# Raw rows into the tensor engine, with weights centred on chip, and a fourth block in the prologue of a two-layer attention and mixture-of-experts kernel

## The chip, the cores and the metric

The kernel runs on one NeuronCore of a Trainium2 chip. Times are device microseconds (us) of one execution. The kernel was run three times, and the median of such runs is what is compared. One further execution was recorded by the hardware profiler; its own time stands beside the median in the table below.

The engines are named as in the profile: PE is the tensor engine (PEld is its weight load), DVE the vector engine, ACT the scalar engine, POOL GpSimd, SP the sync engine. Transfers are issued by SP (the queue SPq) and by POOL.

## The reference

The input x has 128 graphs of 64 nodes with 256 features, in f32: 8192 rows. Two layers follow each other, each of an attention over a graph and a mixture of experts. Cut to what is computed (`ln` is a layer norm without gain and bias):

```python
for l in (0, 1):
    # attention inside each graph, adj is 0/1
    t  = ln(x)                                   # rows of 256
    Wh = t @ W[l]
    e  = (Wh @ a1[l])[:, :, None] + (Wh @ a2[l])[:, None, :]
    if l == 1: e = where(e > 0, e, 0.2 * e)
    p  = softmax(where(adj > 0, e, -9e15))
    x  = x + elu(p @ Wh)
    # mixture of experts: 8 experts, 2 for each row
    t  = ln(x)
    logits = t @ Wr[l]                           # l == 1: + bg + bias
    weights, chosen = softmax over the two largest logits
    act, hidden = (gelu, 256) if l == 0 else (relu, 512)
    f = sum over the two: weight * (act(t @ w1[e] + b1[e]) @ w2[e] + b2[e])
    x = x + (t + f if l == 0 else f)
```

## The kernel before, in words

*Tiling.* The 8192 rows are 16 blocks of 512. A block lies in memory as 128 partitions x 4 tiles (TT) x 256. A layer has 16 such blocks, so there are 32 block steps; block 3 of layer 0 is called FIRST.

*Attention of a block* is a generator, `attend` (L258), which is advanced a step at a time. It takes the statistics of the rows (`ln_stats` L221: mean and variance on DVE, then rs = (var + eps)^-0.5 on POOL, L230), turns adj into an additive mask on POOL (cap, L277), writes the normalised rows xn (`ln_apply` L233: nb = -mean * rs on DVE, L236, then one ACTIVATE for each of the four tiles, L238), transposes xn on PE (`transposed` L243, pt L249; the copies to SBUF are on DVE, L253, and ACT, L255), multiplies by the weights (pw, L288, copied to wh by ACT, L295), and forms scores (pe, L307), the softmax and its transpose (ee, exp, erc, pp, pT, L321 to L340), the product with wh (po, L346) and x + elu (xb, L360). The weights gw have 258 columns: 256 of W, and W @ a1 and W @ a2, which `make_gw` (L164) computes on chip from W and the attention vectors.

*Routing of a block* is a second generator, `route` (L400): statistics of xb, the normalised rows tn (L406), their transpose, the logits (pl, L417; lg, L426), the two largest (`largest` L367, used twice), an exp for the two weights (q), then the row's place in its expert's list (c1 to ix, L456 to L492; before the plan, pn), and eight list writes on POOL (L497), each of which scatters rows of tn with their place into the list of an expert in DRAM. In layer 0 the routine also turns xb into x + t in place, with rs1 = rs + 1 (L433), and stores it as `mid` from POOL's queue (L437); in layer 1 the same line stores xb to the output. The weighted sums of the experts are added to these stores later.

*Experts.* `Slots` works on slots of 256 list rows: `fetch` (L602) issues the load of list rows (xg, L609) and behind it the load of the expert's weights (wc, L651 to L659) on SP's queue; `x` (L669) transposes the rows (px L680, xT L684), `h` (L734) is the first product and its activation (ph L749, hT L757), `y` (L765) the second (py L777, ys L785), and a scatter of its rows to `res` (L791). In layer 1 `weighted` (L807) adds to the output in DRAM. The method `ahead` issues loads of weights ahead of their slot.

*Order.* The order on SP, PE, DVE and ACT is the program's order, written out by hand; only POOL's is chosen by a scheduler. The prologue (L885 to L922) loads blocks 0 to 2, and then advances several `chains` (L897) in turns, one step of each chain a turn; a tuple (turn, steps) tells from which turn on a chain takes part. `load(FIRST)` comes at turn 6, two further loads at turns 8 and 11, and `make_gw(1)` at turn 11:

```python
    chains = [
        (0, att(0)[3:] + [(r, 0)] * 10),
        (1, att(1)[2:] + [(r, 1)] * 10),
        (2, att(2) + [(r, 2)] * 10),
        (11, att(FIRST) + [(r, FIRST)] * 2),
        (20, [(a, FIRST + 1)] * 3),
    ]
```

Then `slots.fetch()` asks for the first list rows, and a loop (L924 to L978) runs over the block steps from FIRST on. An iteration t interleaves the attention of block t + 1 (`a(n)`), the routing of block t (`r(t)`) and four slots (`h`, `x`, `y`). At its first turn the loop gathers the second layer's expert biases (`gather_biases`, `put_biases`), and in the first two turns it fills the tails of the lists with pads (`rest_of_lists` L846, pads L850, eight DMAs for each layer). In layer 0, the lists hold three blocks before the first slot is worked on, so 24 list rows are written on POOL ahead of the first fetch.

Of the kernel before, what the change touches and what calls it, by code (L numbers as in the profile page):

```python
# [16 lines left out]
P = 128  # L17
# [18 lines left out]
def adj_ffn_kernel(  # L36
# [72 lines left out]
    sums_t = [mid_t, out_t]  # L109
# [14 lines left out]
    for g in range(2):  # L124
        r = slice(g * NG, (g + 1) * NG)
        nc.gpsimd.memset(same[r, r], 1.0)
    nhalf = const.tile([P, TT], F32, name="nhalf")
# [35 lines left out]

    def make_gw(l):  # L164
        wt = work.tile([P, KD, D], F32, tag="xt", name=f"wt{l}", bufs=2)
        for o in range(KD):
            pt = ps_c.tile([P, D], F32, tag="a", name=f"pwt{l}_{o}")
            for k in range(KD):
                nc.tensor.transpose(
                    pt[:, k * P : (k + 1) * P], gw[l][:, k, o * P : (o + 1) * P], ident  # L170
                )
            nc.scalar.copy(wt[:, o, :], pt)
        for k in range(KD):
            pa = ps_c.tile([P, 2], F32, tag="a", name=f"pa{l}_{k}")
            for o in range(KD):
                nc.tensor.matmul(
                    pa,
                    lhsT=wt[:, o, k * P : (k + 1) * P],
                    rhs=av[l][:, o, :],
                    start=(o == 0),  # L180
                    stop=(o == KD - 1),
                )
            nc.scalar.copy(gw[l][:, k, D : D + 2], pa)

# [9 lines left out]
    def counted(name, shape, pattern, base, mult):  # L194
        ti = work.tile(shape, I32, tag="cap", name=f"{name}_i")
        nc.gpsimd.iota(ti, pattern=pattern, base=base, channel_multiplier=mult)
        t = const.tile(shape, F32, name=name)
        nc.vector.tensor_copy(t, ti)
        return t
# [21 lines left out]
    def ln_stats(xb, name):  # L221
        st = small.tile([P, TT, 6], F32, tag="st", name=f"st_{name}")
        mv = small.tile([P, TT, 2], F32, tag="mv", name=f"mv_{name}", bufs=4)
# [5 lines left out]
        rs = small.tile([P, TT], F32, tag="rs", name=f"rs_{name}", bufs=4)  # L229
# [3 lines left out]
    def ln_apply(xb, stats, outs, name):  # L233
        mv, rs = stats
        nb = small.tile([P, TT], F32, tag="nb", name=f"nb_{name}", bufs=4)
# [22 lines left out]
    def attend(l, b, blk):  # L258
# [20 lines left out]
        xn = work.tile([P, TT, D], F32, tag="xn", name=f"xn_{name}", bufs=2)  # L279
        ln_apply(xs, stats, lambda t: xn[:, t, :], name)  # L280
        yield
        xt = transposed(xn, "xt", "a", name, l == 0 and b < FIRST)
        yield
        wh = work.tile([P, TT, D + 2], F32, tag="wh", name=f"wh_{name}")
        for t in range(TT):
# [9 lines left out]
            nc.scalar.copy(wh[:, t, :], pw)  # L295
# [71 lines left out]
    def largest(lg, name):  # L367

        mx = small.tile([P, TT], F32, tag="mx", name=f"mx_{name}", bufs=4)
# [8 lines left out]
        mo = small.tile([P, TT], F32, tag="mo", name=f"mo_{name}", bufs=4)  # L378
        nc.vector.tensor_reduce(mo, eq, AX.X, ALU.max)
        oh = small.tile([P, TT, E], F32, tag="oh", name=f"oh_{name}", bufs=4)  # L380
# [19 lines left out]
    def route(l, b, blk):  # L400
# [5 lines left out]
        tn = work.tile([P, TT, ROW[1]], F32, tag="tn", name=f"tn_{name}")  # L406
        nb = ln_apply(xb, stats, lambda t: tn[:, t, 0:D], name)
        if l == 0:
            rs1 = small.tile([P, TT], F32, tag="rs1", name=f"rs1_{name}")
            nc.vector.tensor_scalar(rs1, stats[1], 1.0, None, ALU.add)  # L410
        yield
        tT = transposed(tn, "tT", "r", name, l == 0 and b < FIRST)
# [12 lines left out]
        if l == 0:  # L425
            nc.vector.tensor_copy(lg, pl)  # L426
        else:
            nc.vector.tensor_tensor(lg, pl, gb2[:, 0:1, :].to_broadcast([P, TT, E]), ALU.add)
            nc.vector.tensor_tensor(lg, lg, gb2[:, 1:2, :].to_broadcast([P, TT, E]), ALU.add)
        m1, o1, oh1 = largest(lg, f"{name}a")  # L430
        if l == 0:
            for t in range(TT):
                nc.scalar.activation(  # L433
                    xb[:, t, :], xb[:, t, :], AF.Identity, bias=nb[:, t : t + 1],
                    scale=rs1[:, t : t + 1],
                )
        ins = nc.gpsimd.dma_start(out=sums_t[l][b], in_=xb)  # L437
        if l == 1:
            unordered("sums", ins)
            summed.append(ins)  # L440
# [9 lines left out]
        nc.scalar.activation(q, q, AF.Exp)  # L450
        yield
# [379 lines left out]
    def load_block(l, b, first=None):  # L831

        xs = work.tile([P, TT, D], F32, tag="xs", name=f"xs{l}_{b}")
# [40 lines left out]
    def r(i, n=1):  # L874
# [14 lines left out]
    a(0, 2)  # L889
    make_gw(0)  # L890
    a(0)
    a(1, 2)
# [3 lines left out]
    att = lambda b: [(a, b)] * 9 + [(a, b, 2), (a, b)]  # L896
    chains = [  # L897
        (0, att(0)[3:] + [(r, 0)] * 10),
        (1, att(1)[2:] + [(r, 1)] * 10),
        (2, att(2) + [(r, 2)] * 10),  # L900
        (11, att(FIRST) + [(r, FIRST)] * 2),
        (20, [(a, FIRST + 1)] * 3),
    ]
    turn = 0
    while any(c for _, c in chains):
# [4 lines left out]
        if turn == 2:  # L910
# [3 lines left out]
            tb0 = gather_biases(0)  # L914
        if turn == 5:
            put_biases(0, tb0)
            load_gw(1)
        if turn in (6, 8, 11):
            load(FIRST + (turn - 6) // 2)
        if turn == 11:  # L920
            make_gw(1)
        turn += 1  # L922
    slots.fetch()
    for t in range(FIRST, len(blks)):  # L924
# [4 lines left out]
        if t == FIRST:  # L929
            put_biases(1, gather_biases(1))  # L930
            rest_of_lists(0)
        if t == FIRST + 1:
            rest_of_lists(1)
# [11 lines left out]
        a(n)  # L945
        r(t)
# [20 lines left out]
        r(n)  # L967
        y()
        a(t + 2)
# [5 lines left out]
        r(n)  # L975
# [60 lines left out]
```

## Time and profile before

| | |
|---|---|
| median of 3 runs | 1467.6 us |
| lowest and highest of them | 1464.61 and 1468.28 us |
| the profiled execution | 1464.47 us |
| its span | 1462.6 us |
| its mean granted TensorE clock | 0.956 |
| busy: PE, PEld | 1264.9 us (86%), 1082.9 us (74%) |
| busy: DVE, ACT, POOL | 885.6 us (61%), 670.3 us (46%), 767.8 us (52%) |
| ACTIVATE xn (L238), 128 times | 66.4 us of ACT, 589 ns each |
| ACTIVATE tn (L238), 128 times | 66.4 us of ACT, 589 ns each |
| copy to wh (L295), 128 times | 47.7 us of ACT, 374 ns each |
| list writes (L497), 256 times | 249.5 us of POOL, 975 ns each |

The span is the time from the first to the last recorded instruction. A busy share is an average over the prologue, the loop of layer 0, the loop of layer 1 and the end. The page cuts the span into 40 slices of 36.6 us and gives a digit for each engine: the tenths of the slice in which it was busy. The row PEclk gives in the same way the clock that PE was granted, in tenths of full speed. In an answer of the trace, a line such as "94.31 3.36 PE L346 MATMUL ... x8 [0.21 <-ACT pT_bd L340]" reads: starts at 94.31 us, lasts 3.36 us, line 346, eight of them, after 0.21 us of idle time that ended with an instruction of ACT on pT_bd at line 340. The suffix _g marks a tile of attention, _r one of routing, _s one of a slot.

### The profile page before, as it was taken

The page shows a single profiled execution, that of the slowest core. Times are in us where ns is not written, and L with a number is a line of the kernel's source. Part 1 is how long each engine was busy: PE and PEld are TensorE (multiplying, and loading weights), DVE is VectorE, ACT ScalarE, POOL GpSimd, SP SyncE. Part 2 cuts the span into 40 slices and gives each one's busy share as a digit, 9 for nine tenths or more (in the row PEclk, how much of TensorE's full clock was granted, in tenths as well). Part 3 has the DMA queues.
Part 4 walks back from the last instruction along what each step waited for, and adds up shares of the span by engine and source line. Part 5 has one row for each costly group of instructions (what it writes and reads, how often), then busy time and mean ns, then how long its engine had stood idle before and what let it go on. Part 6 is the DMA issues. An engine that isn't in the chain of part 4 may idle for free. (4 is left out here: it accounts for less than half of the span.)

```text
span 1462.6 us, 22822 instructions
## 1 busy us (share of the span) xinstructions
PE 1264.9 (86%) x6436; PEld 1082.9 (74%) x6436; DVE 885.6 (61%) x3404; ACT 670.3 (46%) x1567; POOL 767.8 (52%) x742
## 2 busy tenths in 40 slices
PE   6646789889989888888889999899988998899996
PEld 4534677777777777777778887777877787688885
DVE  3663777776677678677766655666566655423332
ACT  5523556546655554545444444344444443233232
POOL 3261566656565555555563654555645465544333
PEclk9766999989999999999999999999999999999999
DMA  4228766697666779777786987898877778987773
GB/s 128 83 98 266 240 209 219 210 279 233 214 216 210 268 253 271 260 240 235 240 254 183 265 238 205 220 263 223 228 195 215 209 193 212 241 248 215 214 178 57
DMA packets 267199, 315.42 MB, mean 216 GB/s; under 512 B 41400, under 2 KB 224319, under 8 KB 267073
## 3 DMA queue, kind: packets, MB, share of 16 engines
q1 hardware_dynamic: 222240, 227.80, 51.3%
q0 software_dynamic: 44832, 86.17, 22.0%
q8 instruction: 51, 0.84, 0.2%
q14 instruction: 76, 0.61, 0.1%
HBM read 215.03 MB, written 102.51 MB: 217 GB/s over the span
## 5 line engine op out<-in xcount | busy, mean ns | idle before, releaser
L749 PE MATMUL ph_s<-xT_s,wc_s 128*128 128x256 f32 x1760 | 418.9, 388 | 71.1 <-DVE xT_s L684 49.3
L749 PEld LDWEIGHTS ph_s<-xT_s,wc_s 128*128 128x128 f32 x1760 | 333.4, 193 | 135.1 <-DVE xT_s L684 66.6
L777 PE MATMUL py_s<-wc_s,hT_s 128*128 128x256 f32 x1760 | 417.1, 387 | 14.9 <-issue 14.6
L777 PEld LDWEIGHTS py_s<-wc_s,hT_s 128*128 128x128 f32 x1760 | 331.4, 193 | 59.9 <-issue 17.2
L820 POOL DMA_INDIRECT out_dram<-ys_s,to_s x142 | 223.1, 1571 | 273.2 <-ACT ys_s L817 170.3
L497 POOL DMA_INDIRECT lists<-tn_r,ix_r x256 | 249.5, 975 | 110.9 <-issue 66.1
L757 ACT ACTIVATE hT_s<-ph_s,wc_s 128x256 f32<-128x256 f32 x440 | 182.3, 469 | 176.8 <-PE ph_s L749 88.1
L785 DVE TENSOR_TENSOR ys_s<-py_s,wc_s 128x512 f32<-128x512 f32 x149 | 102.9, 691 | 196.1 <-PE py_s L777 184.5
L791 POOL DMA_INDIRECT res<-ys_s,to_s x156 | 159.0, 1019 | 117.4 <-DVE ys_s L785 51.6
L684 DVE COPY xT_s<-px_s 128x512 f32<-128x512 f32 x149 | 102.3, 686 | 118.1 <-PE px_s L680 118.1
L817 ACT ACTIVATE ys_s<-ys_s,cf_s 128x256 f32<-128x256 f32 x142 | 64.1, 499 | 141.1 <-DVE ys_s L785 134.8
L288 PE MATMUL pw_g<-gw,xt_g 128*128 128x258 f32 x512 | 125.5, 395 | 1.7 <-ACT wh_g L295 1.3
L288 PEld LDWEIGHTS pw_g<-gw,xt_g 128*128 128x128 f32 x512 | 95.8, 196 | 22.8 <-ACT xt_g L255 6.3
L238 ACT ACTIVATE xn_g<-xs,nb_g,rs_g 128x256 f32<-128x256 f32 x128 | 66.4, 589 | 82.0 <-DVE nb_g L236 82.0
L238 ACT ACTIVATE tn_r<-xb_g,nb_r,rs_r 128x256 f32<-128x256 f32 x128 | 66.4, 589 | 66.8 <-DVE nb_r L236 66.8
L680 PE MATMUL px_s<-ident,xg_s 128*128 128x128 f32 x596 | 90.9, 276 | 0.5 <-DMA xg_s<-lists 0.5
L680 PEld LDWEIGHTS px_s<-ident,xg_s 128*128 128x128 f32 x596 | 74.9, 145 | 13.0 <-DMA xg_s<-lists 0.6
L277 POOL TENSOR_SCALAR cap_g<-adj 128x256 f32<-128x256 int32 x32 | 35.7, 1117 | 91.6 <-DMA adj<-in_adj_dram 90.2
L346 PE MATMUL po_g<-wh_g,pT_bd 128*128 128x256 f32 x256 | 69.0, 417 | 7.4 <-ACT pT_bd L340 5.8
L295 ACT COPY wh_g<-pw_g 128x258 f32<-128x258 f32 x128 | 47.7, 374 | 54.2 <-PE pw_g L288 53.2
L417 PEld LDWEIGHTS pl_r<-rw,xt_r 128*128 128x128 f32 x512 | 68.1, 207 | 2.9 <-DVE xt_r L253 0.6
L230 POOL TENSOR_TENSOR rs_r<-ve_r,nhalf 128x4 f32<-128x4 f32 x32 | 38.3, 1198 | 57.1 <-DVE ve_r L228 50.4
(474 smaller groups left out, 1597.8 us busy)
## 6 DMA issues: line engine op xcount, KB each, us to landing
wc_s<-in_w_dram SPq DMA_DIRECT2D x142, 512.0 KB, 4.3
wc_s<-in_w_dram SPq DMA_DIRECT2D x156, 256.0 KB, 3.9
xg_s<-lists SPq DMA_DIRECT2D x78, 258.0 KB, 4.3
xg_s<-lists SPq DMA_DIRECT2D x71, 260.0 KB, 4.4
yb<-res SPq DMA_DIRECT2D x16, 1024.0 KB, 10.5
wc_s<-bcat SPq DMA_DIRECT2D x78, 129.0 KB, 3.8
wc_s<-bcat SPq DMA_DIRECT2D x71, 130.0 KB, 5.3
xs<-in_x_dram SPq DMA_DIRECT2D x16, 512.0 KB, 6.1
```

Source lines behind the costliest of these rows:

```text
L238: nc.scalar.activation(outs(t), xb[:, t, :], AF.Identity, bias=nb[:, t : t + 1], scale=rs[:, t : t + 1])
L288: nc.tensor.matmul(pw, lhsT=xt[:, k, t * P : (t + 1) * P], rhs=gw[l][:, k, :], start=(k == 0), stop=(k == KD - 1),)
L346: nc.tensor.matmul(po[h][:, j, :], lhsT=pT[:, 2 * h + j, :], rhs=wh[:, 2 * h + j, 0:D], start=True, stop=True,)
L497: ins = nc.gpsimd.indirect_dma_start(out=lists[l], out_offset=bass.IndirectOffsetOnAxis(ap=ix[:, k, t : t + 1], axis=0), in_=tn[:, t, 0 : ...
L680: nc.tensor.transpose(px[:, c, t * P : (t + 1) * P], xg[:, t, c * P : (c + 1) * P], ident)
L684: nc.vector.tensor_copy(xT, px)
L749: nc.tensor.matmul(ph[:, j, :], lhsT=wc[:, o : o + P], rhs=xT[:, c, :], start=(c == 0), stop=(c == KD - 1),)
L757: nc.scalar.activation(hT[:, f + j, :], ph[:, j, :], AF.Gelu if l == 0 else AF.Relu, bias=wc[:, OB1[l] + f + j : OB1[l] + f + j + 1],)
L777: nc.tensor.matmul(py[:, t, :], lhsT=hT[:, f, t * P : (t + 1) * P], rhs=wc[:, O2[l] + f * D : O2[l] + (f + 1) * D], start=(f == 0), stop=( ...
L785: nc.vector.tensor_tensor(ys, py, wc[:, OB2[l] : OB1[l]].unsqueeze(1).to_broadcast([P, ST, D]), ALU.add)
L791: ins = nc.gpsimd.indirect_dma_start(out=res[sl["part"]], out_offset=self.row(sl, t), in_=ys[:, t, :], in_offset=None, bounds_check=2 * N - 1,
L820: ins = nc.gpsimd.indirect_dma_start(out=out, out_offset=self.row(sl, t), in_=ys[:, t, :], in_offset=None, compute_op=ALU.add,)
```

## The change

A layer norm followed by a product, ((x - mean) * rs) @ W, equals rs * (x @ (W - column means of W)), since subtracting the row's mean from x is the same as taking each column's mean out of W. The changed kernel uses this form for the attention's product and for the router's.

- A new function `centred` takes the column means out of a weight: two matmuls with a constant matrix `mean` that holds 1/256, and a subtraction on DVE for each of the two halves of the weight. It is applied to gw (with its two columns of attention vectors) and to rw, in both layers.
- In `attend` xn and its nb are gone; the raw rows xs are transposed. The copy to wh becomes an ACTIVATE that multiplies by rs.
- In `route` the raw rows xb are transposed; the logits are multiplied by rs when they are read from PSUM. tn is still made, since the lists hold it, but after the logits. The update of xb and the store of mid come after the exp of q.
- Some small tiles have six buffers instead of four; the integer tile of `counted` uses another tag.
- Block FIRST of layer 0 is loaded with the first three, into a buffer of tag yb, which layer 0 otherwise leaves unused.
- The prologue's chains are written anew: their steps are shorter, blocks 1 and 2 go together, block 3 begins at turn 8 and block 4 at turn 12. The biases of layer 1, the pads of both layers, `make_gw(1)` and the centring of layer 1 are in the prologue, and `slots.ahead()` follows the first fetch.
- In the loop the steps are arranged to the new lengths of `attend` (11 instead of 12) and `route` (11 instead of 10).

```diff
+    mean = const.tile([P, P], F32, name="mean")
+    nc.gpsimd.memset(mean, 1.0 / D)
...
+    def centred(w, n, name):
+        pm = ps_c.tile([P, n], F32, tag="a", name=f"pm_{name}")
+        for k in range(KD):
+            nc.tensor.matmul(pm, lhsT=mean, rhs=w[:, k, :], start=(k == 0), stop=(k == KD - 1))
+        for k in range(KD):
+            nc.vector.tensor_tensor(w[:, k, :], w[:, k, :], pm, ALU.subtract)
...
     def make_gw(l):
...
+        centred(gw[l], D + 2, f"gw{l}")
...
     def attend(l, b, blk):
...
-        xn = work.tile([P, TT, D], F32, tag="xn", name=f"xn_{name}", bufs=2)
-        ln_apply(xs, stats, lambda t: xn[:, t, :], name)
-        yield
-        xt = transposed(xn, "xt", "a", name, l == 0 and b < FIRST)
+        xt = transposed(xs, "xt", "a", name, l == 0 and b < FIRST)
...
-            nc.scalar.copy(wh[:, t, :], pw)
+            nc.scalar.activation(wh[:, t, :], pw, AF.Identity, scale=stats[1][:, t : t + 1])
...
     def route(l, b, blk):
...
-        tn = work.tile([P, TT, ROW[1]], F32, tag="tn", name=f"tn_{name}")
-        nb = ln_apply(xb, stats, lambda t: tn[:, t, 0:D], name)
-        if l == 0:
-            rs1 = small.tile([P, TT], F32, tag="rs1", name=f"rs1_{name}")
-            nc.vector.tensor_scalar(rs1, stats[1], 1.0, None, ALU.add)
-        yield
-        tT = transposed(tn, "tT", "r", name, l == 0 and b < FIRST)
+        tT = transposed(xb, "tT", "r", name, l == 0 and b < FIRST)
...
-        if l == 0:
-            nc.vector.tensor_copy(lg, pl)
-        else:
-            nc.vector.tensor_tensor(lg, pl, gb2[:, 0:1, :].to_broadcast([P, TT, E]), ALU.add)
-            nc.vector.tensor_tensor(lg, lg, gb2[:, 1:2, :].to_broadcast([P, TT, E]), ALU.add)
+        nc.vector.tensor_tensor(
+            lg, pl, stats[1].unsqueeze(2).to_broadcast([P, TT, E]), ALU.mult
+        )
+        for i in range(2 * l):
+            nc.vector.tensor_tensor(
+                lg, lg, gb2[:, i : i + 1, :].to_broadcast([P, TT, E]), ALU.add
+            )
         m1, o1, oh1 = largest(lg, f"{name}a")
-        if l == 0:
-            for t in range(TT):
-                nc.scalar.activation(
-                    xb[:, t, :], xb[:, t, :], AF.Identity, bias=nb[:, t : t + 1],
-                    scale=rs1[:, t : t + 1],
-                )
-        ins = nc.gpsimd.dma_start(out=sums_t[l][b], in_=xb)
+        yield
+        tn = work.tile([P, TT, ROW[1]], F32, tag="tn", name=f"tn_{name}")
+        nb = ln_apply(xb, stats, lambda t: tn[:, t, 0:D], name)
         if l == 1:
+            ins = nc.gpsimd.dma_start(out=out_t[b], in_=xb)
             unordered("sums", ins)
             summed.append(ins)
         yield
...
         nc.scalar.activation(q, q, AF.Exp)
+        yield
+        if l == 0:
+            rs1 = small.tile([P, TT], F32, tag="rs1", name=f"rs1_{name}")
+            nc.vector.tensor_scalar(rs1, stats[1], 1.0, None, ALU.add)
+            for t in range(TT):
+                nc.scalar.activation(
+                    xb[:, t, :], xb[:, t, :], AF.Identity, bias=nb[:, t : t + 1],
+                    scale=rs1[:, t : t + 1],
+                )
+            nc.gpsimd.dma_start(out=mid_t[b], in_=xb)
         yield
...
+        tag, bufs = ("yb", 2) if l == 0 and b == FIRST else ("xs", 3)
+        xs = work.tile([P, TT, D], F32, tag=tag, name=f"xs{l}_{b}", bufs=bufs)
...
     load_router()
-    a(0, 2)
+    load(FIRST)
+    a(0, 3)
     make_gw(0)
-    a(0)
-    a(1, 2)
+    centred(rw[0], E, "rw0")
+    a(1, 3)
...
-    att = lambda b: [(a, b)] * 9 + [(a, b, 2), (a, b)]
+    att = lambda b: [(a, b, 2)] + [(a, b)] * 6 + [(a, b, 2), (a, b)]
+    rou = lambda b: [(r, b, 2), (r, b, 2)] + [(r, b)] * 6
     chains = [
-        (0, att(0)[3:] + [(r, 0)] * 10),
-        (1, att(1)[2:] + [(r, 1)] * 10),
-        (2, att(2) + [(r, 2)] * 10),
-        (11, att(FIRST) + [(r, FIRST)] * 2),
-        (20, [(a, FIRST + 1)] * 3),
+        (0, att(0)[2:] + rou(0)),
+        (2, att(1)[2:] + rou(1)),
+        (2, att(2) + rou(2)),
+        (8, att(3) + [(r, 3)]),
+        (12, [(a, 4, 2)]),
     ]
...
         if turn == 5:
-            put_biases(0, tb0)
+            put_biases(0, tb)
             load_gw(1)
-        if turn in (6, 8, 11):
-            load(FIRST + (turn - 6) // 2)
+            tb = gather_biases(1)
+            put_biases(1, tb)
+        if turn in (6, 8):
+            load(4 + (turn - 6) // 2)
         if turn == 11:
             make_gw(1)
+            centred(rw[1], E, "rw1")
+            for l in range(2):
+                rest_of_lists(l)
         turn += 1
+    r(2)
     slots.fetch()
+    slots.ahead()
     for t in range(FIRST, len(blks)):
...
-        if t == FIRST:
-            put_biases(1, gather_biases(1))
-            rest_of_lists(0)
-        if t == FIRST + 1:
-            rest_of_lists(1)
...
         if more:
             x()
         a(n)
+        r(t)
         r(t)
...
         r(n)
+        r(t)
         y()
-        a(t + 2)
         r(t)
         r(t)
         y()
         slots.fetch()
         x()
-        r(n)
         r(t)
```

More of the change, by code (lines that the diff above doesn't have):

```diff
@@ L108, in adj_ffn_kernel @@
     res_t = [r.rearrange("(b t p k) d -> b p t (k d)", t=TT, p=P, k=2) for r in res]
-    sums_t = [mid_t, out_t]
     def part(b):
@@ L194, in counted @@
     def counted(name, shape, pattern, base, mult):
-        ti = work.tile(shape, I32, tag="cap", name=f"{name}_i")
+        ti = work.tile(shape, I32, tag="ee", name=f"{name}_i")
         nc.gpsimd.iota(ti, pattern=pattern, base=base, channel_multiplier=mult)
@@ L222, in ln_stats @@
         st = small.tile([P, TT, 6], F32, tag="st", name=f"st_{name}")
-        mv = small.tile([P, TT, 2], F32, tag="mv", name=f"mv_{name}", bufs=4)
+        mv = small.tile([P, TT, 2], F32, tag="mv", name=f"mv_{name}", bufs=6)
         for t in range(TT):
@@ L228, in ln_stats @@
         nc.vector.tensor_scalar(ve, mv[:, :, 1], LN_EPS, None, ALU.add)
-        rs = small.tile([P, TT], F32, tag="rs", name=f"rs_{name}", bufs=4)
+        rs = small.tile([P, TT], F32, tag="rs", name=f"rs_{name}", bufs=6)
         nc.gpsimd.tensor_tensor(rs, ve, nhalf, ALU.pow)
@@ L234, in ln_apply @@
         mv, rs = stats
-        nb = small.tile([P, TT], F32, tag="nb", name=f"nb_{name}", bufs=4)
+        nb = small.tile([P, TT], F32, tag="nb", name=f"nb_{name}", bufs=6)
         nc.vector.scalar_tensor_tensor(nb, mv[:, :, 0], -1.0, rs, ALU.mult, ALU.mult)
@@ L367, in largest @@
     def largest(lg, name):
-        mx = small.tile([P, TT], F32, tag="mx", name=f"mx_{name}", bufs=4)
+        mx = small.tile([P, TT], F32, tag="mx", name=f"mx_{name}", bufs=6)
         nc.vector.tensor_reduce(mx, lg, AX.X, ALU.max)
@@ L377, in largest @@
         )
-        mo = small.tile([P, TT], F32, tag="mo", name=f"mo_{name}", bufs=4)
+        mo = small.tile([P, TT], F32, tag="mo", name=f"mo_{name}", bufs=6)
         nc.vector.tensor_reduce(mo, eq, AX.X, ALU.max)
-        oh = small.tile([P, TT, E], F32, tag="oh", name=f"oh_{name}", bufs=4)
+        oh = small.tile([P, TT, E], F32, tag="oh", name=f"oh_{name}", bufs=6)
         nc.vector.tensor_tensor(
@@ L831, in load_block @@
     def load_block(l, b, first=None):
-        xs = work.tile([P, TT, D], F32, tag="xs", name=f"xs{l}_{b}")
+        tag, bufs = ("yb", 2) if l == 0 and b == FIRST else ("xs", 3)
+        xs = work.tile([P, TT, D], F32, tag=tag, name=f"xs{l}_{b}", bufs=bufs)
         yb = None
@@ L913, in adj_ffn_kernel @@
             snum = counted("snum", [P, SF], [[1, SF]], 0, 0)
-            tb0 = gather_biases(0)
+            tb = gather_biases(0)
         if turn == 5:
-            put_biases(0, tb0)
+            put_biases(0, tb)
             load_gw(1)
-        if turn in (6, 8, 11):
-            load(FIRST + (turn - 6) // 2)
+            tb = gather_biases(1)
+            put_biases(1, tb)
+        if turn in (6, 8):
+            load(4 + (turn - 6) // 2)
         if turn == 11:
             make_gw(1)
+            centred(rw[1], E, "rw1")
+            for l in range(2):
+                rest_of_lists(l)
         turn += 1
+    r(2)
     slots.fetch()
+    slots.ahead()
     for t in range(FIRST, len(blks)):
```

## The prediction, made before the changed kernel had run

> **What bounds the kernel now.** I read the page's share of busy time and its 40 slices first, then busy time by window, then the tensor engine's waits, then the order of time around the longest of them.
>
> ```profile
> PE 1264.9 (86%) x6436; PEld 1082.9 (74%) x6436; DVE 885.6 (61%) x3404; ACT 670.3 (46%) x1567; POOL 767.8 (52%) x742
> ...
> PE   6646789889989888888889999899988998899996
> ...
> PEclk9766999989999999999999999999999999999999
> ```
>
> PE is the bound, but not at the start: the first four slices (146 us) hold digits 6, 6, 4, 6 and a granted clock that falls to 0.6. The windows say it in figures (columns: window, length, then busy us of PE, PEld, DVE, ACT, POOL, clock, DMA share, GB/s):
>
> ```profile
> 60.00:80.00 20.00, 14.64 (x62) 11.97 (x63) 13.53 (x69) 10.58 (x24) 5.92 (x6) 0.57 0.21 66
> 80.00:100.00 20.00, 10.78 (x51) 8.73 (x49) 11.00 (x51) 6.18 (x19) 15.43 (x17) 0.74 0.36 126
> 100.00:120.00 20.00, 8.67 (x29) 6.02 (x30) 8.89 (x44) 5.92 (x13) 9.22 (x10) 0.57 0.53 159
> 120.00:140.00 20.00, 10.02 (x45) 7.50 (x43) 9.57 (x34) 5.84 (x19) 3.00 (x3) 0.61 0.94 280
> ```
>
> No engine is full here; the prologue is a chain of waits. Of the 198 us in which PE is idle (1462.6 - 1264.9), 65 lie before 200 us, by the same windows added up from 0. Its waits up to 200 us (line waited at, what it waited for, total, times, longest):
>
> ```profile
> PE pt_g L249 <- ACT xn_g L238: 26.1, 9, 13.6
> ...
> PE ph_s L749 <- DMA wc_s<-in_w_dram: 6.4, 1, 6.4
> PE pwt L169 <- DMA gw<-in_gnn_w_dram: 6.1, 1, 6.1
> ```
>
> 26.1 is also the total of that first wait over the whole run: after 200 us PE never waits for a normalised row. The place of the longest two, in order of time:
>
> ```profile
> 94.31 3.36 PE L346 MATMUL po_g<-wh_g,pT_bd 128*128 128x256 f32 x8 [0.21 <-ACT pT_bd L340]
> 111.28 2.80 PE L249 MATMUL pt_g<-ident,xn_g 128*128 128x128 f32 x8 [13.60 <-ACT xn_g L238]
> ...
> 123.41 0.63 PE L680 MATMUL px_s<-ident,xg_s 128*128 128x128 f32 x4
> ...
> 138.66 3.38 PE L749 MATMUL ph_s<-xT_s,wc_s 128*128 128x256 f32 x8 [6.40 <-DMA wc_s<-in_w_dram]
> ```
>
> Why 13.6: the scale rs of block 4 is ready to be made at 102.4, but POOL is writing list rows, 24 of them from 77.72 to 109.32 at 0.96 + 0.30 us each, and rs stands behind. Why 6.4: the sync queue issues the first expert's weights at 134.15, behind a bias gather that holds it to 123.15 and eight pads of 9.29 us:
>
> ```profile
> 110.99 3.07 SPq L609 DMA_DIRECT2D xg_s<-lists  x4
> ...
> 123.65 9.29 SPq L850 DMA_DIRECT2D lists<-pad  x8
> 134.15 0.40 SPq L651 DMA_DIRECT2D wc_s<-in_w_dram  x1
> ```
>
> **The change, step by step.** The sum is made against the profiled execution (1464.47 us, of it 1462.6 span); the median of the runs is 1467.6, 3.1 more, and that is added at the end. PE's order in the loop is the same list of matmuls as before; only the prologue's order differs.
>
> *Loop.* Removed: 128 ACTIVATEs (xn, 589 ns, 66.4 us of ACT) and 32 nb (152 ns) on DVE. Added: the copy to wh (374 ns) becomes a scaled ACTIVATE from PSUM. No row shows that; bounds are 374 and 589 (L238, two operands from SBUF), nearest is L757 (PSUM, one pointer operand, 469 ns): +95 ns x 128 = 12 us of ACT. PE hides both: a tile of pw takes it 0.87 us, in which ACT spends 0.5 us waiting, and after 200 us no xn wait is left to win. Without that cover it would be 0.4 us per block. The router's scale replaces a copy of 0.19 us by a multiply of the same size; nb_r now stands ahead of ys and erc on DVE, at most 0.15 us in the roughly 20 blocks where PE waits for the softmax: +2. The update of xb and the store of mid move two steps later; mid is read again only in layer 1, and the transposes no longer wait for tn, so nobody is late. Loop: +2 us (0 to +5; the freed ACT could give back up to 5).
>
> *Start.* The first transposes need only x: 5.2 instead of 9.81 us. But the first weights must be centred before any pw: 4 matmuls like pw (395 ns, 1.6) and 2 subtractions like L321 (0.42, 0.85), after the attention vectors. So pw starts at about 12.7 (12.43 now). Gained is what followed: block 1's transposes no longer wait for xn, so pe of block 0 comes at 17.5 instead of 21.0, pw of block 2 at 27 instead of 35.9, the first router logits at 44 instead of 55.5.
>
> *The list chain.* The first expert row can be fetched only after 24 list rows are written, and they start with ix of block 0. In the new DVE order ix of block 0 stands behind nearly all else: from xb of block 0 (35.2) come 36.6 us of DVE work (5 statistics of 2.4, for r0, g3, r1, r2, g4; 5 half routings of 1.35 to 1.7; xb of three blocks at 2.6; the rest in pieces under 1 us; 2.75 for ix itself). DVE stalls on top: it must wait for block 1's logits, which queue on PE behind block 3's transposes, these behind a PSUM bank that DVE frees late (4 us); for the centring of layer 1, which POOL's and ACT's queues don't hide because DVE's subtraction stands in line behind sm of block 3 (pw, ACT's xb and xt copies, wt, scores, 4 matmuls: 7.5 us); some 2 more. 35.2 + 36.6 + 13.5 = 85.3, with signal hops 86, against 77.7 now. Bounds: 76 with half those stalls and some overlap, 92 with twice the centring stall.
>
> [...] after the 13.6 us gap the half-rate matmuls last from 111.28 to 119.5 (pw 5.67 instead of 3.83), and the windows from 60 to 140 stay at 0.57 to 0.74. I take the rows: 3.42, 1.7, 3.42, and 86.
>
> From there POOL: 24 x 1.27, two stores of mid (0.85) and one rs (1.05) = 33.3, end at 119.3 (109.3 now). Fetch 1.7 later as now, landing 4.4 us after (section 6), so px at 125.4 (123.4 now). Block 4's rs is ahead of the list rows in the new POOL order, so the 13.6 us wait goes, but PE arrives early and waits for xg: that is the next late thing.
>
> *The weights.* They follow xg directly: 119.3 + 1.7 + 3.1 + 1.6, landing 4.3 later at 130. From px to the first ph the chain of pp, po takes 8.8 (123.4 to 132.25 now): 134. So ph starts at 134 instead of 138.66: -5. The 6.4 us are won, 1.4 are lost by the later lists. Pads, bias gather and loads now stand earlier on the sync queue, behind the load of block 5 (its buffer comes free near 43 us); 16 pads of 1.16 end near 62, long before the first list row that waits for them.
>
> *Second stall.* At 171.97 PE waits 5.2 us for xn of block 6. That goes; but the next ph needs weights issued at 172.29, landing 4.3 later, and ran at 179.81: at most 3.2 is won, and mid of block 3 now lies among the list rows (-0.9): -2.3. Clock recovered in both stalls: -2 (0 to -4).
>
> Sum: +2 - 5 - 2.3 - 2 = -7.3, so 1457 for the profiled execution and 1460 for the median. The ends: list start at 76 gives -10 more (1450), at 92 gives +6 (1466).
>
> **Rivals.** *Dense prologue and freed ACT*: list start near 76, ACT's 54 us help the loop by 5: 1460 - 10 - 5 = 1445 at best, 1449 as its middle. For it: no engine is above 77% in any window from 60 to 140 us. Against: DVE alone has 36.6 us of work in that stretch. *Traded*: the new wait for xg takes the place of both old ones, list start at 89: 1464 to 1471, like now; for it speaks that POOL's 31 us of list rows are unchanged. *Slower*: the centring of layer 1 sits in DVE's line; if its stall is 20 us instead of 7.5, list start is 98, ph at 146 and the second gain can't cover it: 1460 + 13 = 1473. It decides from a list start of 95 on. Against it: make_gw alone took 2.5 us at 60 us.
>
> **How the numbers follow.** Likeliest (1453 to 1463): 0.47. Dense: 0.19. Traded: 0.20. Slower: 0.14. Three runs spread by 3.7 us, so 0.3% (4.4 us) is about what can be told. Below 1463.2 lie the first two: faster 0.66; traded is mostly same: 0.19; slower with a piece of traded: 0.15. The range 1446 to 1472 leaves out half of the slower case and a third of the dense one.
>
> **What would show it.** Right: no wait for xn; the first list row near 86 and the last near 119; px waiting for xg by 8 to 14 us; no wait for weights; first ph near 134; loop iterations as long as before (38 us); DVE idle for 7 us ahead of the subtraction of layer 1. Wrong: a first list row before 80 or after 92, or loop waits of ph and pp that differ by more than 5 us in sum.

## The result, and the profile after

The changed kernel takes 1463.02 us (median of 20 runs, 1458.29 to 1468.07), the kernel before 1467.19 us (20 runs, 1462.14 to 1471.29). The ratio is 0.9971, interval 0.9960 to 0.9982: 4.2 us faster, between 2.6 and 5.9. The profiled executions stand closer together, 1464.47 and 1462.60 us, since that of before lies 2.7 us below its own median and that of after 0.4 us below. Where traces are subtracted below, this is why they sum to less than the medians.

The page of the changed kernel, the rows that answer to those of before:

```profile
PE 1264.8 (87%) x6452; PEld 1088.8 (75%) x6452; DVE 887.3 (61%) x3396; ACT 627.8 (43%) x1439; POOL 765.9 (52%) x743
...
PE   7746788889899888888899999889988898899996
...
PEclk9757999999999998999999999999999999999999
```

ACT lost 42.5 us of work (670.3 to 627.8) and PE is as busy as before: the freed ACT time did not shorten PE's (e2 below tells what it was worth). The copy to wh, now scaled, takes 476 ns, close to the 469 taken for it. The first four slices of PE read 7, 7, 4, 6 instead of 6, 6, 4, 6. The windows from 60 to 140 us (same columns as before):

```profile
60.00:80.00 20.00, 17.12 (x72) 14.59 (x72) 8.97 (x44) 7.86 (x20) 2.18 (x2) 0.67 0.30 90
80.00:100.00 20.00, 7.53 (x33) 6.06 (x31) 14.69 (x74) 9.33 (x25) 12.34 (x13) 0.67 0.26 92
100.00:120.00 20.00, 9.10 (x44) 7.70 (x44) 8.98 (x42) 6.00 (x17) 14.81 (x16) 0.67 0.34 119
120.00:140.00 20.00, 13.01 (x48) 10.39 (x48) 11.03 (x40) 5.34 (x11) 1.63 (x2) 0.66 0.85 250
```

PE is busy 46.8 us of these 80, against 44.1 before: the prologue is still a chain of waits, only with other names. PE's waits up to 200 us:

```profile
PE px_s L691 <- DMA xg_s<-lists: 10.2, 2, 8.1
PE pw_g L296 <- DVE xt_g L264: 10.1, 1, 10.1
PE ph_s L760 <- DVE xT_s L695: 7.7, 4, 5.4
PE pp_g L345 <- DVE c_r L467: 6.9, 1, 6.9
```

No row for xn and none for the weights is left. In their place PE waits for DVE's line (10.1 and 6.9) and, as the last long wait ahead of the first ph, for the first list rows (8.1). The places where the prediction put numbers, on POOL, SP and PE:

```profile
85.65 1.12 POOL L508 DMA_INDIRECT lists<-tn_r,ix_r  x1 [1.17 <-DVE l_r L444]
...
117.71 0.96 POOL L508 DMA_INDIRECT lists<-tn_r,ix_r  x1 [0.30 <-issue]
```

```profile
46.58 13.20 SPq L863 DMA_DIRECT2D lists<-pad  x16
...
120.62 3.09 SPq L620 DMA_DIRECT2D xg_s<-lists  x4
124.26 0.38 SPq L662 DMA_DIRECT2D wc_s<-in_w_dram  x1
```

```profile
123.48 1.12 PE L691 MATMUL px_s<-ident,xg_s 128*128 128x128 f32 x4 [8.10 <-DMA xg_s<-lists]
...
131.33 2.94 PE L760 MATMUL ph_s<-xT_s,wc_s 128*128 128x256 f32 x8
```

The weights follow the first fetch by 3.6 us (23.2 before: 110.99 to 134.15), the first ph runs at 131.33 instead of 138.66. The first list row, however, is written at 85.65 instead of 77.72.

### The profile page after: what moved, and what is told of

The parts are those of the page before. It is cut to its first block, busy times and chain, and to the rows that moved or that the text cites. A ratio compares the mean times of both kernels' runs of the same rounds, so it can differ in the third digit from the quotient of the medians.

```text
span 1460.7 us, 22860 instructions
## 1 busy us (share of the span) xinstructions
PE 1264.8 (87%) x6452; PEld 1088.8 (75%) x6452; DVE 887.3 (61%) x3396; ACT 627.8 (43%) x1439; POOL 765.9 (52%) x743
## 3 DMA queue, kind: packets, MB, share of 16 engines
q0 software_dynamic: 44832, 86.17, 22.2%
## 5 line engine op out<-in xcount | busy, mean ns | idle before, releaser
L788 PE MATMUL py_s<-wc_s,hT_s 128*128 128x256 f32 x1760 | 421.5, 390 | 14.3 <-issue 11.2
L296 PE MATMUL pw_g<-gw,xt_g 128*128 128x258 f32 x512 | 124.0, 395 | 12.5 <-DVE xt_g L264 10.1
L691 PE MATMUL px_s<-ident,xg_s 128*128 128x128 f32 x596 | 92.2, 278 | 10.2 <-DMA xg_s<-lists 10.2
L303 ACT ACTIVATE wh_g<-pw_g,rs_g 128x258 f32<-128x258 f32 x128 | 60.6, 476 | 65.7 <-PE pw_g L296 64.3
L345 PE MATMUL pp_g<-ident,ee_g 128*64 128x128 f32 x128 | 20.8, 289 | 52.1 <-DVE ee_g L341 26.5
```

The lines of the kernel that those rows point to most:

```text
L296: nc.tensor.matmul(pw, lhsT=xt[:, k, t * P : (t + 1) * P], rhs=gw[l][:, k, :], start=(k == 0), stop=(k == KD - 1),)
L691: nc.tensor.transpose(px[:, c, t * P : (t + 1) * P], xg[:, t, c * P : (c + 1) * P], ident)
L788: nc.tensor.matmul(py[:, t, :], lhsT=hT[:, f, t * P : (t + 1) * P], rhs=wc[:, O2[l] + f * D : O2[l] + (f + 1) * D], start=(f == 0), stop=( ...
```

## The experiments

All ratios are to the kernel before, run on the same chip in the same stretch; the changed kernel's is 0.9971.

### One half alone: the prologue, the loop

*e1* has the changed prologue and the loop of before (shown as the difference between the two forms of the functions; the kernel holds both and picks by block):

```diff
     # attend, blocks from 4 on
+        xn = work.tile([P, TT, D], F32, tag="xn", name=f"xn_{name}", bufs=2)
+        ln_apply(xs, stats, lambda t: xn[:, t, :], name)
+        yield
-        xt = transposed(xs, "xt", "a", name, l == 0 and b < FIRST)
+        xt = transposed(xn, "xt", "a", name, l == 0 and b < FIRST)
...
-            nc.scalar.activation(wh[:, t, :], pw, AF.Identity, scale=stats[1][:, t : t + 1])
+            nc.scalar.copy(wh[:, t, :], pw)
...
     # route, blocks from 3 on: tn first, as before; the loop's order as before
```

> The changed kernel's prologue (weights centred, raw rows, block 3 early, pads and biases early) with the loop of before: from block 4's attention and block 3's routing on, xn and tn are made first and transposed, as before. Theory (the gain is all in the prologue and the loop gives 2 to 4 us back): first ph near 131, loop as before, 5 to 8 us faster than before, so 1460. Rival (the ACT time freed in the loop is the gain): within 2 us of before.

Measured: 0.9924 (0.9906 to 0.9943), 1457.96 against 1469.26 us, 11 us faster. The gain is in the prologue, and it is larger without the new loop: 11 us where 5 to 8 were expected. The place of the first ph was missed as well: it ran at 136.0, because block 4's xn was waited for once more (12.4 us).

*e2* is the other half: prologue of before, loop of the change, both layers' weights centred at the head of the loop:

```diff
     # attend for blocks 0 to 3 and route for blocks 0 to 2 as before
...
         if t == FIRST:
             put_biases(1, gather_biases(1))
             rest_of_lists(0)
+            for l in range(2):
+                centred(gw[l], D + 2, f"gw{l}")
+                centred(rw[l], E, f"rw{l}")
```

> The prologue of before (its order, its loads, xn and tn for blocks 0 to 2, xn for block 3) with the loop of the changed kernel on raw rows; the weights of both layers are centred at the head of the loop, where PE was idle 13.6 us. Theory: first ph stays near 138.7 since the weights' loads still stand behind the pads; the wait for xn of block 4 goes but nothing starts earlier; the loop costs 2 to 4 us and the second stall gives up to 3 back: -2 to +3 us against before. Rival (freed ACT): 4 us or more faster.

Measured: 1.0016 (1.0005 to 1.0027), 2.1 us slower. As expected, and against the rival: 35 us less work on ACT (635.5 against 670.3) gained nothing.

### The sync queue

*e3*, the changed kernel with the queue as before:

```diff
         if turn == 5:
...
-            tb = gather_biases(1)
-            put_biases(1, tb)
...
-            for l in range(2):
-                rest_of_lists(l)
...
     slots.fetch()
-    slots.ahead()
     for t in range(FIRST, len(blks)):
...
+        if t == FIRST:
+            put_biases(1, gather_biases(1))
+            rest_of_lists(0)
+        if t == FIRST + 1:
+            rest_of_lists(1)
```

> The changed kernel, but the gather of the second layer's biases and the pads go back to the first two turns of the loop, and the weights are not issued right behind the first fetch. Theory: the weights follow 12 us behind the fetch again, first ph at 138 to 140 instead of 131.3, so 6 to 8 us slower than the changed kernel (1469 to 1471). Rival (list rows and the wait for xg set the start, the queue's order does not): within 2 us of the changed kernel.

Measured: 1.0094 (1.0074 to 1.0114), 1483.02 us. That is 1.2% or 18 us slower than the changed kernel, more than twice what was expected. SP's queue and PE in this run:

```profile
116.46 3.05 SPq L620 DMA_DIRECT2D xg_s<-lists  x4
...
129.85 7.56 SPq L863 DMA_DIRECT2D lists<-pad  x8
138.61 0.39 SPq L662 DMA_DIRECT2D wc_s<-in_w_dram  x1
```

```profile
145.11 3.60 PE L760 MATMUL ph_s<-xT_s,wc_s 128*128 128x256 f32 x8 [17.72 <-DMA wc_s<-in_w_dram]
```

From fetch to weights 22.2 us pass instead of 3.6; the list rows even came 4 us earlier (first at 81.7), and PE just waited longer for the weights. First ph is 13.8 us late. I had counted the pads alone (12 us) and not the gather of the biases ahead of them.

*e7* is the converse, the kernel before with the queue's part alone:

```diff
             load_gw(1)
+            put_biases(1, gather_biases(1))
...
             make_gw(1)
+            for l in range(2):
+                rest_of_lists(l)
         turn += 1
     slots.fetch()
+    slots.ahead()
...
-        if t == FIRST:
-            put_biases(1, gather_biases(1))
-            rest_of_lists(0)
-        if t == FIRST + 1:
-            rest_of_lists(1)
```

> The kernel before with the sync queue's part of the change alone: biases of layer 1 gathered at turn 5, pads of both layers at turn 11, weights issued right behind the first fetch. xn and tn are made first and transposed as before. Theory (6.4 us of the gain at the start are the weights' place in the queue): no wait of ph for the weights, first ph near 132.5 instead of 138.7, 4 to 7 us faster than before, ratio 0.995 to 0.997. Rival (the early pads hold up the list rows or the loads, or the next wait takes the time back): within 2 us of before.

Measured: 0.9946 (0.9930 to 0.9961), 1457.81 against 1466.10 us: 8.3 us faster, a little more than the 4 to 7 expected. Its queue and its PE:

```profile
110.56 3.09 SPq L609 DMA_DIRECT2D xg_s<-lists  x4
114.20 0.38 SPq L651 DMA_DIRECT2D wc_s<-in_w_dram  x1
```

```profile
110.78 2.81 PE L249 MATMUL pt_g<-ident,xn_g 128*128 128x128 f32 x8 [13.60 <-ACT xn_g L238]
...
130.71 2.90 PE L749 MATMUL ph_s<-xT_s,wc_s 128*128 128x256 f32 x8
```

The longest wait of the page of before, 13.60 us, is still there, and yet the first ph is at 130.71, earlier than in the whole change. In the kernel before the weights came later than all that this wait held up.

### The fourth block

*e8* loads block 3 at turn 6 into the old buffers:

```diff
-        tag, bufs = ("yb", 2) if l == 0 and b == FIRST else ("xs", 3)
+        tag, bufs = "xs", 3
...
-    load(FIRST)                       # with the first loads
...
-        if turn in (6, 8):
-            load(4 + (turn - 6) // 2)
+        if turn in (6, 8, 11):
+            load(FIRST + (turn - 6) // 2)
```

> The changed kernel, but block 3 is loaded at turn 6 as before, into the buffers of blocks 0 to 2 (blocks 4 and 5 at turns 8 and 11). Theory (the list chain sets the start; block 3 is first needed at 49 us and would land near 46): within 2 us of the changed kernel, ratio to before 0.9955 to 0.9985; the pads end near 80 instead of 60, still ahead of the first list row at 85. Rival (the early fourth block is what shortens the start): 4 us or more slower than the changed kernel.

Measured: 0.9966 (0.9952 to 0.9979), the changed kernel's 0.9971 within the interval; first ph at 130.8. The early fourth block moves nothing that can be measured; the pads ended at 72.6, where 80 was expected.

### The centring of layer 1

*e4*:

```diff
         if turn == 11:
-            make_gw(1)
-            centred(rw[1], E, "rw1")
...
     slots.ahead()
+    make_gw(1)
+    centred(rw[1], E, "rw1")
```

> The changed kernel, but the attention vectors and the centring of layer 1 come after the first fetch instead of at turn 11. Theory (the subtraction's stall stands in DVE's line ahead of ix of block 0): DVE's wait of 5.9 us at 68 to 74 goes, list rows start at 78 to 80 instead of 85.7 and end near 112, first ph near 125: 5 to 7 us faster than the changed kernel (1457). Rival (another wait takes its place on DVE): list rows start after 83, within 2 us of the changed kernel.

Measured: 0.9922 (0.9903 to 0.9940), 1456.66 against 1469.26 us; 0.5% or 7 us better than the change. In the changed kernel DVE's line showed the stall, in e4 POOL and PE show what it was worth:

```profile
74.16 0.76 DVE L172 TENSOR_TENSOR gw<-gw,pm_gw 128x258 f32<-128x258 f32 x2 [5.87 <-PE pm_gw L170]
```

```profile
79.71 1.12 POOL L508 DMA_INDIRECT lists<-tn_r,ix_r  x1 [1.17 <-DVE l_r L444]
```

```profile
124.95 2.57 PE L760 MATMUL ph_s<-xT_s,wc_s 128*128 128x256 f32 x8
```

5.9 us of stall gone, the first list row 5.9 us earlier, the first ph 6.4.

### The loop's loss

Cut at the start of po in four block steps (5, 15, 21 and 24, then 31), the traces give these lengths in us; A is layer 0, B the change of layers, C and D layer 1:

| kernel | A: 5 to 15 | B: 15 to 21 | C: 21 to 24 | D: 24 to 31 | sum |
|---|---|---|---|---|---|
| before | 330.2 | 238.0 | 148.4 | 318.8 | 1035.4 |
| e7 (loop of before) | 330.0 | 240.6 | 148.5 | 318.6 | 1037.7 |
| e1 (loop of before) | 327.2 | 240.1 | 148.4 | 318.8 | 1034.5 |
| changed | 327.1 | 242.4 | 148.4 | 323.8 | 1041.7 |
| e2 (loop of the change) | 327.3 | 241.9 | 148.8 | 322.1 | 1040.1 |
| e4 (loop of the change) | 327.0 | 242.2 | 148.6 | 323.9 | 1041.7 |
| e5 | 329.8 | 240.3 | 148.7 | 320.1 | 1038.9 |
| e12 | 321.0 | 242.1 | 149.1 | 314.8 | 1027.0 |

The old loop has 1035.9 on the mean, the new one 1041.2 (e3 1043.0 and e8 1041.7 agree): 5 us lost, most of it in D. The medians leave the size open: e2, the new loop with the old prologue, is 2.1 us slower than before (0.7 to 4.0), while e1, the old loop with the new prologue, is 6.9 us faster than the changed kernel. In D PE waits once in each step for the softmax. The waits of PE behind 878 us in the changed kernel, and behind 885 us in the kernel before:

```profile
PE pp_g L345 <- DVE ee_g L341: 18.6, 7, 3.0
```

```profile
PE pp_g L337 <- DVE ee_g L333: 17.0, 7, 2.7
```

DVE in one such step, changed kernel, then before:

```profile
1056.74 0.19 DVE L427 TENSOR_TENSOR lg_r<-pl_r,rs_r 128x32 f32<-128x32 f32 x1
1056.96 0.53 DVE L431 TENSOR_TENSOR lg_r<-lg_r,gb 128x32 f32<-128x32 f32 x2
...
1058.53 0.16 DVE L247 SCALAR_TENSOR_TENSOR nb_r<-mv_r,rs_r 128x4 f32<-128x4 f32 x1
1058.60 3.75 DVE L276 SCALAR_TENSOR_TENSOR xs<-yb,cs,xs 128x256 f32<-128x256 f32 x8
```

```profile
1060.74 0.19 DVE L428 TENSOR_TENSOR lg_r<-pl_r,gb 128x32 f32<-128x32 f32 x1
1060.97 0.19 DVE L429 TENSOR_TENSOR lg_r<-lg_r,gb 128x32 f32<-128x32 f32 x1
...
1062.38 3.75 DVE L265 SCALAR_TENSOR_TENSOR xs<-yb,cs,xs 128x256 f32<-128x256 f32 x8
```

From the first lg to the start of the long row it is 1.86 us now and 1.64 before in this pair of steps; in most steps of layer 1 it is 1.75 and 1.45. Of these 0.30 us one more operation on the logits is 0.23 (as from 1060.74 to 1060.97), and nb ahead of the row 0.07 (1058.53 to 1058.60). pp waits 2.9 to 3.0 us instead of 2.5 to 2.7 in six of the steps, 1.6 us in all. The rest of the 5.0 us is PE itself: the same 1503 matmuls take 293.9 us instead of 290.5. The next step of the changed kernel shows how:

```profile
1108.63 0.60 PE L345 MATMUL pp_g<-ident,ee_g 128*64 128x128 f32 x4 [2.90 <-DVE ee_g L341]
1109.07 5.30 PE L788 MATMUL py_s<-wc_s,hT_s 128*128 128x256 f32 x16
```

The same 16 matmuls take 3.62 us at 1155.74, after a wait of 2.90 us as well. The granted clock accounts for the 3.4 us: in D it is 0.50 for one stretch of 3.41 us in before (from 1022.13) and for three in the changed kernel (from 925.34, 973.12 and 1109.66), and each costs about 1.7 us (5.30 - 3.62). Steps of D drawn out in this way number one in before and e7 (old loop), three in the changed kernel, two in e8 and two in e5, whose waits are back at 2.6 to 2.8 us. PE's busy time in D, 290.5 us in before and 293.9 in the changed kernel, is 290.4 in e1 (old loop), 292.2 in e2, 293.7 in e3 and 293.8 in e4; at 1.7 us a step, an estimate, that is one, two, three and three.

*e5* takes the two additions out of the line:

```diff
-        for i in range(2 * l):
-            nc.vector.tensor_tensor(
-                lg, lg, gb2[:, i : i + 1, :].to_broadcast([P, TT, E]), ALU.add
-            )
+        if l == 1:
+            nc.vector.tensor_tensor(lg, lg, gb2[:, 0:1, :].to_broadcast([P, TT, E]), ALU.add)
...
+    nc.vector.tensor_tensor(gb2[:, 0, :], gb2[:, 0, :], gb2[:, 1, :], ALU.add)
...
         r(t)
-        r(t)
         if t + 2 != NB:
             a(t + 2)
         y()
         a(n)
+        r(t)
```

> The changed kernel with the two additions to DVE's line ahead of the softmax taken out again: the router's two biases are added to each other once, so layer 1 has a multiply and one add in place of the two adds of before, and nb with tn comes behind the softmax's step. Theory (in layer 1 the loop loses 0.3 us a block at the wait of pp for ee, 3.0 us instead of 2.7, and the longer wait draws the half clock more often, 3 of the last 7 steps instead of 1, at 1.7 us each): waits of pp for ee back to 2.7 us, layer 1 steps back to 44.7, 4 to 8 us faster than the changed kernel, ratio to before 0.9925 to 0.9945. Rival (the loss in layer 1 comes with the raw transposes or the later store): within 2 us of the changed kernel.

Measured: 0.9969 (0.9956 to 0.9982), nothing gained on the changed kernel's 0.9971. In layer 1 it did most of what it should (D 320.1, waits 17.0 us in 7, but two steps drawn out where one was expected), but in layer 0 it made a wait of its own. PE's waits from 300 to 500 us:

```profile
PE po_g L354 <- ACT pT_bd L348: 9.5, 6, 1.8
```

This row has 0.8 us in the changed kernel: with nb later, the four ACTIVATEs of tn come later too, and the copy of the probabilities queues behind them on ACT. The edit was two in one, and only its layer 1 half tells something.

*e6* moves the long row instead:

```diff
-        if t + 2 != NB:
-            a(t + 2)             # layer 1: eight instructions, 3.75 us
         y()
         a(n)
...
         y()
-        a(t + 2, 1 + (t + 2 == NB))
+        a(t + 2, 2)
```

> The changed kernel, but the eight DVE instructions (3.75 us) that add the experts' outputs to the rows of block t+2 in layer 1 come behind the second y of the iteration instead of ahead of the softmax of block t+1. Theory (they are what pp waits for in layer 1): the 3.0 us waits of pp for ee go in the last 7 steps (19 us) and the half clock after them with them (5 us); 15 to 25 us faster than the changed kernel, ratio to before 0.980 to 0.987. Rival (the wait moves to ys or xT, which then stand behind the same 3.75 us): within 5 us of the changed kernel.

Measured: 1.0189 (1.0173 to 1.0206), 27 us slower than before and 32 slower than the changed kernel. The rival had the mechanism, a wait that moves to xT, but not its size (within 5 us). pp waits only 1.0 us (6.9 in 7), and the row copy of the next slot stands behind the same work; PE in one step:

```profile
1102.87 5.38 PE L760 MATMUL ph_s<-xT_s,wc_s 128*128 128x256 f32 x16 [3.00 <-issue]
```

The row names no releaser ("issue"), but DVE's copy xT for it began at 1102.09. Such waits take 18.0 us in six steps of D. Most of the loss lies earlier, in C: 166.5 us instead of 148.4, where ph waits 15.8 us for xT instead of 4.9. Behind the copy at 1102.09 and the statistics that follow it, DVE waited 5.0 us for PE (1106.7 to 1111.7): a gap for the row.

### Putting it together

*e9* (e4 with the biases added once), *e10* (e9, and the long row in the gap) and *e11* (e1 with the centring late) were run in a stretch in which the kernel before took 1720.62 us, though on the chip of the same number as e1 to e4, where it had taken 1469.26.

> The changed kernel with the centring of layer 1 behind the first fetch (as in e4) and the router's two biases added to each other once, so that in layer 1 DVE's line ahead of the softmax has one add less (0.23 us of the 0.30 us that it gained); nb and tn stay where the changed kernel has them. Theory: the last 7 steps of layer 1 fall from 45.0 to 44.8 us with one or two of them drawn out by the half clock instead of three: 2 to 5 us faster than e4, ratio to before 0.988 to 0.991. Rival (the clock's hits do not depend on 0.2 us of wait): 0.9915 or above.

> As e9, and in the loop the row copy of the next slot comes ahead of the statistics of block t+2 in layer 0, and in layer 1 the eight DVE instructions that add the experts' outputs to block t+2 (3.75 us) and its statistics (2.3 us) come behind the statistics of block t+1's routing, where DVE waited 5.0 us for PE in e6. Theory (a DVE line is free where PE is the later one): the waits of pp for ee in layer 1 fall to 1.0 us, no new wait above 1 us, last steps near 43 us, ratio to before 0.974 to 0.982. Rival (as in e6 the wait moves to ys or xT behind it): 0.988 or above.

> As e1 (the changed kernel's prologue, the loop of before), with the centring of layer 1 behind the first fetch as in e4. Theory (both gains are of different places and add): first ph near 125, 5 to 7 us faster than e1, ratio to before 0.987 to 0.9895. Rival (in the loop of before block 4's xn, for which PE waited 12 us in e1, holds the start): ratio 0.9915 or above.

Measured: 0.9683 (0.9651 to 0.9714), 0.9564 (0.9538 to 0.9591), 0.9830 (0.9804 to 0.9855). These numbers decide nothing about the theories. ACT and DVE stood still together for over 3 us 23 times in e9, 18 in e10 and 30 in e11 (behind 200 us; 2 times in e4), and for many of their waits there the trace names no releaser in the core ("remote"). DVE's longest such row in e9:

```profile
DVE xt_r L264 <- remote: 98.0, 19, 8.1
```

No such row stands among the DVE waits of e4 or e12. Whether the sums of e1 and e4 add, and what the one bias alone brings, stays open. So the last run was e10's kernel again:

```diff
+        if t + 2 < NB:                # layer 0: statistics, now behind the copy of x()
             a(t + 2)
...
         r(n)
         r(t)
+        if t + 2 >= NB:
+            a(t + 2)                  # layer 1: the long row
         y()
+        if t + 2 >= NB:
+            a(t + 2)                  # its statistics
```

> The kernel of e10 once more. In e9 to e11 DVE and ACT both stood still for 5 to 8 us in most block steps with no releaser named, in before too by its 1720 us, so their ratios carry that. Theory: without it, ratio to before 0.976 to 0.985 (e4's 0.992, less 0.2 to 0.3% for the one bias, less 9 to 17 us for the waits of pp for ee that went from 2.7 to 1.0 us in e10 with 1 to 2 us of new waits in the step, and the clock after them). Rival (the wait only moves, as in e6): 0.988 or above.

Measured: 0.9824 (0.9800 to 0.9848), 1440.40 against 1468.00 us: 27.6 us faster than before and some 21 us (1.5%) faster than the changed kernel (0.9824 / 0.9971 = 0.9853). PE and DVE in one step:

```profile
1043.98 0.60 PE L345 MATMUL pp_g<-ident,ee_g 128*64 128x128 f32 x4 [0.98 <-DVE ee_g L341]
1044.42 3.62 PE L786 MATMUL py_s<-wc_s,hT_s 128*128 128x256 f32 x16
...
1062.68 3.69 PE L786 MATMUL py_s<-wc_s,hT_s 128*128 128x256 f32 x16 [0.69 <-issue]
```

```profile
1058.23 3.75 DVE L276 SCALAR_TENSOR_TENSOR xs<-yb,cs,xs 128x256 f32<-128x256 f32 x8
```

The long row now runs while PE has 3.6 us of py, pp waits 0.98 us, py behind it takes 3.62 us. D is 314.8 us; new waits of 0.69 and 1.18 us in the step keep it from more. Behind pp, py takes 3.62 us in every step of D: none is drawn out. A is 6.0 us shorter than in e4, 4.7 of them idle time of PE (ph's waits for xT fall from 21.6 to 17.2 us): the row copy no longer stands behind the statistics. Against the changed kernel, the trace is 6.5 us shorter up to po of block 5 (6.8 in e4), 14.7 in the loop and 1.2 behind it.

## Why the prediction was right, and where it was not

The forecast was 7.3 us faster for the trace and 1460 for the median. It is 4.2 us by the medians and 1.9 by the two traces: inside the range, the sign right, but 1463.02 lies at the upper edge of the likeliest stretch (1453 to 1463), and 0.29% is just short of the 0.3% that the forecast held to be about the least that can be told. By the traces 7.9 us are won up to po of block 5 (168.5 to 160.6), 6.3 are lost in the loop and 0.3 won behind it; the sum had 9.3 won by start, second stall and clock, and 2 lost.

*The start: right in its result.* First list row 86, measured 85.65; last row's end 119.3, measured 118.67 (117.71 + 0.96); px 125.4, measured 123.48; first ph 134, measured 131.33. The gain there is 7.3 us where the sum had 5: the rows landed 2.9 us after their issue, not 4.4 (123.48 - 120.62), and px to ph took 7.85 us, not 8.8. DVE's stall ahead of the subtraction was 5.87 us where 7.5 were taken. That 85.3 was met so closely is in part luck: from 35.2 to 85.35 DVE worked 32.5 us and stood still 17.6, where the sum had 36.6 of work and 13.5 of stalls. e4 shows that this stall carried through one to one to the list rows. The early rows of the sum were less good: first pw 15.10 (12.7), pe of block 0 21.00 (17.5), which is where it was before; ahead of pw stand the transposes of block 1, which I had not counted. The first logits came at 43.35 all the same (44 predicted).

*The clock there.* The step took the rates of the rows of before, half rate on the chain, and that was right for all three groups. (In before itself the clock is 0.50 from 100.53 to 117.60, 1.9 us short of the 119.5 that the prediction gives.) Second and third logits took 3.42 and 3.56 us, and the four wide matmuls of the centring between them 2.07 us, where eight of this width took 2.01 us at full clock (pw at 65.30). The granted clock was 0.50 while PE worked 8.73 us without a break:

```profile
72.05:80.78 8.73, 8.73 (x34) 7.86 (x33) 3.19 (x18) 1.27 (x5) 0.00 (x0) 0.50 0.13 46
```

The list start of 85.65 lies next to the 86 that these rates gave.

*The second stall: the mechanism was only half of it.* The wait for xn went as said, but ph of the second stall moved from 179.81 to 171.95, 0.6 us more than the first ph, where 2.3 were forecast. The larger gain at the start (7.3 where 5 were forecast) made up for it, which as far as the sum goes is luck. Two waits took its place, the next rows at 164.99 (2.1 us) and then DVE's line:

```profile
171.95 3.78 PE L760 MATMUL ph_s<-xT_s,wc_s 128*128 128x256 f32 x8 [5.43 <-DVE xT_s L695]
```

The copy xT (171.22) stood behind statistics, x + elu, statistics and the list places of block 4, 10 us almost without a break.

*The loop: the step that was mis-sized.* "Loop: +2 us (0 to +5)". By the segments it is 5.3 (1041.2 - 1035.9), just over the upper bound; by the medians of e2 it may be less. I had written that the scale "replaces a copy of 0.19 us by a multiply of the same size". That holds in layer 0, where a copy went. In layer 1 there was no copy: an add went to the multiply's place and a second add was needed, so the line grew by one operation in each block, 0.23 us, and by nb, 0.07, just where PE waits for the softmax: 0.30 us where at most 0.15 had been counted. The second half of the size is the clock: I had given the two stalls a clock gain of 2 us and given the longer waits of the loop no clock loss; measured are 3.4 us of PE time in D. Shown is one drawn-out step in before and e7, and two or three in the changed kernel, e5 and e8. That the 0.3 us of longer wait bring the difference is not shown, since e5 has two with the shorter wait (the last section takes up single waits). The gain of 3 us in A is the clock's too: between blocks 9 and 10 PE waits 2.3 us for sm in before and 2.6 in the changed kernel, then the granted clock is 0.50 for 10.2 us (315.57 to 325.81) in before and for 3.4 (310.94 to 314.35) in the changed kernel, and the step takes 37.6 and 35.0 us. In e7 it takes 37.6, in e5 35.2 and in e8 35.0. No run ties that to the raw rows; e1 has the shorter A (327.2) with the old loop.

*What the change was worth, by part.* The queue alone gives 0.54% (e7), the fourth block nothing (e8), the raw rows in the loop cost (e2), and the centring of layer 1 in DVE's line costs another 0.5% (e4). What the raw rows bring in the prologue alone no run tells; e1, which has them with the queue, has 0.76%, and its interval overlaps with that of e7. The prediction had the queue at "6.4 are won, 1.4 are lost by the later lists"; that trade is what e7 and e4 show from both sides. The rival *traded* was thus true of the lists, not of the sum.

## What to carry to other kernels

Look for the last wait of a stage, not its longest: a wait of 13.6 us could stay, and the gain came from 20 us of queue between a fetch and its weights. When a normalisation is folded into weights, count the operations it adds on each engine in each branch, and put the folding itself where no line of work waits behind it (5.9 us of stall in DVE's line put the first list row 5.9 us later, e4). And before moving a row out of one wait, find the gap on its engine in which it is to run: the same 3.75 us made the changed kernel some 32 us slower in one place (e6, 1.0189 / 0.9971) and are part of the 21 us won in another (e12).

## What had not been expected of the hardware

In D PE was slower behind some waits of 2.61 (e7) to 3.14 us (e8), with 16 matmuls in 4.8 to 5.3 us instead of 3.62, not behind each: three of six in the changed kernel and one of six in before, there with a granted clock of 0.50. In these two traces the changes of the granted clock lie whole multiples of 3.41 us apart, to within 0.01 us. Counted in steps of 3.41 us from the first instruction, they fall 1.54 us into a step in before and 0.32 in the changed kernel. Two waits of 2.90 us in D of the changed kernel, in stretches of 3.41 us laid from such a change (columns as before), the first with the half clock behind it, the second without:

```profile
1106.24:1109.65 3.41, 1.02 (x7) 0.99 (x8) 3.27 (x12) 0.00 (x0) 0.00 (x0) 1.00 0.41 129
1109.65:1113.06 3.41, 3.41 (x10) 2.71 (x9) 1.51 (x8) 1.27 (x3) 0.52 (x1) 0.50 0.94 333
```

```profile
1150.61:1154.02 3.41, 1.80 (x11) 1.35 (x9) 3.27 (x9) 1.91 (x4) 0.00 (x0) 1.00 0.09 31
1154.02:1157.44 3.42, 2.13 (x12) 1.98 (x13) 3.15 (x15) 0.00 (x0) 0.00 (x0) 1.00 0.50 69
1157.44:1160.85 3.41, 3.41 (x17) 2.99 (x17) 1.99 (x7) 1.85 (x4) 1.54 (x1) 1.00 0.79 282
```

The first leaves PE idle for 2.4 us of one stretch, the second for 1.6 and 1.3 us of two. Before and the changed kernel have 12 waits of pp of over 2 us in D: the half clock followed the 4 that left PE idle for 2.14 to 3.01 us of one stretch, and none of the 8 that left it idle for at most 1.88. The seven waits of 0.98 us in e12 had py at 3.62 us behind them. In layer 0 idle time does not part the stretches so: in the changed kernel the half clock followed one with 0.61 us of it (from 307.52), while the clock stayed full behind one with 2.00 (from 304.11). What sets the clock is not shown.

In e9 to e11 ACT and DVE stopped together 18 to 30 times for over 3 us, the longest time in e9 for 7.1, which goes with a kernel before that was 17% slower in that stretch (1720.62 against 1468.00 us); what they waited for, the traces do not name.
